# Depthwise convolution by stacks in both layers, a second tile for the sums made on GpSimd, and a third bank of exponentials ahead of a long activation

## The chip, the cores and the metric

The kernel runs on one core of a Trainium2 chip. All eight images of the batch are worked on by this one core, one after the other. The metric is device time in microseconds; the runs shown are three, and their median is what the change is measured against. One further execution was profiled, and everything said below of single instructions is from that one.

The engines are named as in the profile: PE is the matrix engine (TensorE), PEld its weight loads, DVE is VectorE, ACT is ScalarE, POOL is GpSimd, SP is the engine that issues the DMAs.

## The reference, cut to what matters

The input is eight images of 56 x 56 points with 192 channels, in float32. Each layer adds its result to its input, and each is applied to a group norm of its input (32 groups of 6 channels).

```python
# layer 0: attention on separable convolutions
x = x + L0(gn(x))
#   q  = pointwise(batchnorm(depthwise3x3(xn, dw_q,  stride 1)))      3136 queries
#   kv = pointwise(batchnorm(depthwise3x3(xn, dw_kv, stride 2)))       784 keys
#   o  = softmax(q k^T / 8) v     (3 heads of 64), then out_w, out_b

# layer 1: a selective scan in four directions
x = x + L1(gn(x))
#   xa, z = split(xn @ in_proj)                 384 channels each
#   xc = silu(depthwise3x3(xa) + conv_b)
#   for four directions k (rows, columns, and both reversed):
#     dt, B, C = split(xs @ x_proj[k]);  delta = softplus(dt @ dt_proj[k] + bias[k])
#     h = exp(delta * A) * h + delta * B * u     # 384 channels x 16 states, 3136 points
#     y = sum over the 16 states of h * C
#   out = (layernorm(sum of the four y, plus the skip) * silu(z)) @ out_proj
```

## The kernel before, in words

The points of an image are cut into seven chunks of 448 (`T`), that is eight rows of 56. The 384 channels of the scan are three blocks of 128 partitions (`NJ`).

**The scan** is the main loop. A step is one image, one direction and one chunk; there are 8 x 4 x 7 = 224 steps of 16 states each. For each state of a step:

- `inputs_made` (L1165, POOL): h = du x B for 128 x 1344 elements, into one of seven tiles h (`HBUFS`).
- `decays` (L1179, ACT): three exponentials da, each into a PSUM bank.
- `scans` (L1196, DVE): three scans of 448 elements, h = da x h + input; `carries` (L1218) keeps the last column.
- For most states PE turns h round (`turned`, L1242, 12 transposes), ACT scales the result by C (`scaled`, L1258), and PE turns it back into the sum y (`back`, L1276).
- For four states of a step (three in the last image) POOL multiplies by C instead (`by_pool`, L1294) and adds up in a tile `yp` (L1298): two groups of states to a step. PE adds each finished group to y (`summed`, L1313). The tile `yp` exists once; the first product of a group can be written only when PE has read the group before.
- DVE adds y to the image's sum `yacc` (L1330 and L1328).

**What goes before and after an image's scan.** `front(b)` is layer 0 and the beginning of layer 1 for image b. It turns the input round and takes the statistics (L519 to L534), then loads normalised bands of ten rows (L576) and convolves them: `dgkv` and `dgq` are diagonal 96 x 96 matrices, one for each of nine taps and two channel blocks, and each tap is a matmul on the shifted band (L634 for keys and values with 112 columns, L471 for queries with up to 448). The pointwise products follow (L651 to L665), then the attention (`attend`, L775 and L784, with the exponentials at L725), the product with out_w (L756), a second group norm, and the in-projection of layer 1 (L890). Layer 1's depthwise convolution goes by *stacks* (L908): a stack holds the same rows three times, shifted by one image row, on 3 x 32 partitions, so that one matmul with 32 output channels does three taps; four such matmuls, for four groups of 32 channels, write four quarters of the PSUM partitions. A silu over 3136 elements ends it (`stored`, L870). `x_proj(b)` makes delta, B and C (L982 to L999) with one Softplus for every two directions of a chunk (L958). `finish(b)` is the layer norm, the gate with a silu of its own (L1063) and the output product.

**The order of the work.** Each of these is a Python generator that asks for an engine with an estimated cost, what it reads and what it writes. A planner (`Sched.run`) keeps an estimated time for each engine and always takes the request that could start first; what comes out is one fixed order of instructions on each engine, the DMAs on SP's queue among them. All engines take their queues in order. While image b is scanned, `front(b+1)` and `x_proj(b+1)` are woven in; `pace` holds the estimated PE time that they have used to a share that grows with the scans done, within 12 us. When PE has nothing to do by the planner's estimate, it is given filler matmuls (L1408). The front of image 0 stands ahead of the first scan and overlaps with nothing.

**PSUM.** During the scan y takes three banks. Five banks are shared by name: at most two for the exponentials (`rda`), two for turned states (`rht`) and one for everything in `front`, `x_proj` and `finish` (`bank1`).

**Weights** of the pointwise products, of out_w, of x_proj and of dt_proj (`pwq`, `pwkv`, `outw0`, `outw1`, `xpw`, `dtw`) stay in SBUF for the whole run.

Of the kernel before, what the change touches and what calls it, by code (L numbers as in the profile page):

```python
# [18 lines left out]
L = HW * HW  # L19
# [26 lines left out]
LEAD = 3  # L46

# [226 lines left out]
def kernel(  # L274
# [54 lines left out]
    pwq = fill("pwq", [CP, NB, 256], 0.0)  # L329
    nc.sync.dma_start(pwq[:, :, 0:C], pw_q.rearrange("(b p) d -> p b d", p=CP))  # L330
    pwkv = load("pwkv", [CP, NB, 2 * C], pw_kv.rearrange("(b p) d -> p b d", p=CP))
    outw0 = load("outw0", [128, C], out_w[0:128, :])
    outw1 = fill("outw1", [128, C], 0.0)
    nc.sync.dma_start(outw1[0:64, :], out_w[128:192, :])
# [3 lines left out]
    xpw = fill("xpw", [128, 2, NJ, 2, 64], 0.0)  # L338
    for k in range(NDIR):
        nc.sync.dma_start(xpw[:, k % 2, :, k // 2, :NR], xp_wT[k].rearrange("(j p) r -> p j r", p=128))  # L340

    dtw = fill("dtw", [128, NDIR, DIN], 0.0)
    for k in range(NDIR):
        nc.sync.dma_start(dtw[k // 2 * 64:k // 2 * 64 + R, k], dt_wT[:, k, :])
# [37 lines left out]
    dgq_d = dconst.tile([CP, NB, 9, CP], F32, name="dgq_d")  # L382
    dgkv_d = dconst.tile([CP, NB, 9, CP], F32, name="dgkv_d")
    dgx_d = dconst.tile([96, NJ, 4, 3, 32], F32, name="dgx_d")
    xpd = [dconst.tile([128, NJ, HW + 2, HW + 2], F32, name=f"xpd{i}") for i in range(2)]
    for t in xpd:
        for row in (0, HW + 1):
            nc.sync.dma_start(t[:, :, row], zeros[:, :HW + 2].unsqueeze(1).to_broadcast([128, NJ, HW + 2]))
    with tc.tile_pool(name="taps", bufs=2) as taps:
        for dst, src, p, nb in ((dgq_d, dw_q, CP, NB), (dgkv_d, dw_kv, CP, NB)):  # L390
            w = taps.tile([p, nb, 9], F32, name="w")
            nc.sync.dma_start(w, src.rearrange("(b p) t -> p b t", p=p))
            for bl in range(nb):
                d = taps.tile([p, 9, p], F32, name="d")
                for t in range(9):
                    nc.vector.tensor_scalar(d[:, t], ident[:p, :p], w[:, bl, t:t + 1], None, ALU.mult)
                nc.sync.dma_start(dst[:, bl], d)


        id3 = taps.tile([96, 32], F32, name="id3")  # L400
        w3 = taps.tile([96, NJ, 4, 3], F32, name="w3")
        for dy in range(3):
            rows = slice(32 * dy, 32 * dy + 32)
            nc.vector.tensor_copy(id3[rows], ident[rows, rows])
            nc.sync.dma_start(w3[rows].rearrange("c j g x -> c (j g) x"),
                              conv_w[:, 3 * dy:3 * dy + 3].rearrange("(q c) x -> c q x", c=32))
        for j in range(NJ):
            d = taps.tile([96, 4, 3, 32], F32, name="d3")
            for g in range(4):
                for dx in range(3):  # L410
                    nc.vector.tensor_scalar(d[:, g, dx], id3, w3[:, j, g, dx:dx + 1], None, ALU.mult)
            nc.sync.dma_start(dgx_d[:, j], d)
# [4 lines left out]
    s1 = Rings(ctx.enter_context(tc.tile_pool(name="s1", bufs=1)), 1)  # L417
# [44 lines left out]
    TAPS = (4, 0, 1, 2, 3, 5, 6, 7, 8)  # L462

    def conv_rows(out, lhs, img, row0, rows, t):


        dy, dx = divmod(t, 3)
        lo, hi = max(row0 + dy - 1, 0), min(row0 + dy - 1 + rows, HW)
        o0, o1 = lo - (row0 + dy - 1), hi - (row0 + dy - 1)
        a, b = max(0, 1 - dx), min(HW, HW + 1 - dx)  # L470
        nc.tensor.matmul(out[:, o0:o1, a:b], lhs, img(lo, hi)[:, :, a + dx - 1:b + dx - 1],  # L471
                         start=(t == TAPS[0]), stop=(t == TAPS[-1]))

# [18 lines left out]
    def front(b):  # L492
# [13 lines left out]
        with tc.tile_pool(name=f"fx_{b}", bufs=2) as pool:  # L506
            fx = Rings(pool, 2)
            k_st = [Cell() for _ in range(NCH)]

            def part(c):  # L510
# [3 lines left out]
                xt = yield fx("xt", [CP, NB, T], parts=NB)  # L514
# [13 lines left out]
                yield from dma(xt.c, [k_xr[c]], 3.8, xr[:, :, cols], xt.ap, [xt])  # L528
# [5 lines left out]
            nc.vector.scalar_tensor_tensor(off, mean, -1.0, rstd, ALU.mult, ALU.mult)  # L534

        with tc.tile_pool(name=f"kv_{b}", bufs=1) as kvp:
# [18 lines left out]
            with tc.tile_pool(name=f"fd_{b}", bufs=1) as fd:  # L555
                fe = Rings(fd, 1)
                dgq = fd.tile([CP, NB, 9, CP], F32, name="dgq")
                dgkv = fd.tile([CP, NB, 9, CP], F32, name="dgkv")
                k_dq, k_dk = Cell(), Cell()
                yield from dma([], [k_dk], 7.4, dgkv, dgkv_d)  # L560
                yield from dma([], [k_dq], 5.7, dgq, dgq_d)
                s_q, t_q = bns["q"]
                s_kv, t_kv = bns["kv"]
                bands, ends = {}, []

                def load_bands():
                    for c in range(NCH):
                        base = c * RPC - 1
                        r0, r1 = max(base, 0), min(base + BR, HW)
                        band = yield fe("band", [CP, NB, BR, HW], parts=3)  # L570
                        bv = band.ap[:, :, r0 - base:r1 - base]
                        yield from dma(k_xr[max(c - 1, 0):c + 2], [band.c[2]], 4.5, bv,
                                       xr.rearrange("p b (h w) -> p b h w", w=HW)[:, :, r0:r1])
                        for bl in range(NB):
                            yield ACT, t_act(BR * HW), [band.c[2], k_gn], [band.c[bl]]
                            nc.scalar.activation(bv[:, bl], bv[:, bl], AF.Identity, bias=off[:, bl:bl + 1],  # L576
                                                 scale=rstd[:, bl:bl + 1])
                        bands[c] = band
# [37 lines left out]
                def convs():  # L616
                    for c in range(NCH):
                        base = c * RPC - 1
                        yield lambda: c in bands
                        band = bands[c]  # L620


                        hkv = yield fe("hkv", [CP, NB, TP], parts=NB)
                        hq = yield fe("hq", [CP, NB, T], parts=NB)
                        for bl in range(NB):
                            pk = yield bank()
                            pkv = pk.ap[:CP, :TP].rearrange("p (h w) -> p h w", w=KW)
                            for t in range(9):
                                dy, dx = divmod(t, 3)
                                nr = 4 if c * RPC + 6 + dy < HW else 3  # L630
                                ncol = KW if dx < 2 else KW - 1
                                if t % 3 == 0:
                                    yield PE, 3 * t_mm(TP), [band.c[bl], k_dk], pk.c if t == 6 else []
                                nc.tensor.matmul(pkv[:, :nr, :ncol], dgkv[:, bl, t],  # L634
                                                 band.ap[:, bl, 1 + dy:1 + dy + 2 * nr - 1:2, dx:dx + 2 * ncol - 1:2],
                                                 start=(t == 0), stop=(t == 8))
                            sc.spawn(kv_out(pk, hkv, bl))
# [533 lines left out]
    def decays():  # L1171
        for i, n in todo:
# [8 lines left out]
            if n == NST - 1:  # L1181
                dl.free()
# [297 lines left out]
```

## Time and profile before

| | |
|---|---|
| three runs, us | 17917.75, 17898.47, 17909.62; median 17909.62 |
| the profiled execution's own time, us | 17887.45 |
| its span on the core, us | 17885.7 |
| granted PE clock | 0.974 |
| busy, us: PE, DVE, ACT, POOL | 16160.6, 14114.4, 14223.1, 15550.4 |
| PE filler matmuls (L1408), us | 1423.6 |
| first POOL input of the scan, us from the start | 742.2 |
| DMA traffic | 2306.95 MB, 129 GB/s on average |

Three stretches follow one another. Up to about 740 us stands the front of image 0. Then come seven periods, each with the scan of one image and the front of the next; bands are loaded at 11866.5 and again at 14043.5 us, so that a period is some 2170 us long. From about 16,150 us on the last image is scanned with no front beside it. A row of a table of stretches gives the stretch and its length, then the busy time and the number of instructions of PE, PEld, DVE, ACT and POOL, the granted PE clock, the DMA engines' share and the GB/s. A row of waits gives the waiting line, what it waited for, the sum in us, how often, and the longest.

### The profile page before, as it was taken

Reading aid. Unit: us, or ns where it says so; the run is one execution under the profiler, and the core shown is the slowest. Engines: PE = TensorE matmul, PEld = TensorE weight load, DVE = VectorE, ACT = ScalarE, POOL = GpSimd, SP = SyncE. Lnnn points to the kernel's source line nnn. Section 1 sums busy time; section 2 is a strip of 40 time slices with the busy share of each in tenths; the row PEclk is TensorE's granted clock in tenths of the full one; section 3 lists DMA queues with packets and bytes.
Section 4 is the critical chain, followed back from the end, with each engine's and each line's share of the span. In section 5 each row is a group of like instructions: output and inputs, shape, how many; then the busy total and the mean of one; then the engine's idle time right before and its main releaser. Section 6 shows DMA issues by size and latency. Waiting matters only on the chain. (4 is left out here: it accounts for less than half of the span.)

```text
span 17885.7 us, 277600 instructions
## 1 busy us (share of the span) xinstructions
PE 16160.6 (90%) x99800; PEld 11302.8 (63%) x99800; DVE 14114.4 (79%) x17839; ACT 14223.1 (80%) x25030; POOL 15550.4 (87%) x5200
## 2 busy tenths in 40 slices
PE   8699989998899989999899998999989999899998
PEld 4366656666666666666566665666656666667776
DVE  2378878888778887788787887878878788788898
ACT  2478878787877878788787887878878788888888
POOL 0388889898898989899898998989979899899998
PEclk9799999999999999999999999999999999999999
DMA  1643365334553355533554336543364433643332
GB/s 51 183 151 93 101 182 168 108 99 123 173 165 97 95 140 166 158 99 98 155 156 152 100 97 168 155 139 102 95 179 155 129 100 98 190 151 115 95 100 79
DMA packets 1461825, 2306.95 MB, mean 129 GB/s; under 512 B 189264, under 2 KB 1447776, under 8 KB 1457376
## 3 DMA queue, kind: packets, MB, share of 16 engines
q1 hardware_dynamic: 1460448, 2289.19, 43.6%
q8 instruction: 791, 12.96, 0.3%
q14 instruction: 586, 4.80, 0.1%
HBM read 1758.53 MB, written 530.15 MB: 128 GB/s over the span
## 5 line engine op out<-in xcount | busy, mean ns | idle before, releaser
L1196 DVE TENSOR_TENSOR_SCAN h<-da,newc,h 128x448 f32<-128x448 f32 x9216 | 10077.2, 1136 | 1781.7 <-ACT da L1179 1184.3
L1165 POOL TENSOR_TENSOR h<-du_s,bb 128x1344 f32<-128x1344 f32 x3584 | 10818.6, 3052 | 613.8 <-PE ht L1242 502.2
L1258 ACT ACTIVATE g<-ht,ct_s 112x384 f32<-112x384 f32 x10864 | 5928.9, 577 | 1596.5 <-PE ht L1242 1386.1
L1179 ACT ACTIVATE da<-dl_s,acoef 128x448 f32<-128x448 f32 x10752 | 6582.2, 636 | 741.1 <-DVE h L1196 391.6
L1276 PE MATMUL y<-ident,g 112*128 112x112 f32 x32592 | 4865.3, 268 | 649.4 <-ACT g L1258 458.7
L1242 PE MATMUL ht<-ident,h 128*112 128x128 f32 x32592 | 5181.5, 277 | 221.5 <-DVE h L1196 136.2
L1276 PEld LDWEIGHTS y<-ident,g 112*128 112x128 f32 x32592 | 3556.7, 142 | 2648.2 <-ACT g L1258 1569.1
L1242 PEld LDWEIGHTS ht<-ident,h 128*112 128x112 f32 x32592 | 3679.2, 135 | 847.1 <-DVE h L1196 392.8
L1196 DVE TENSOR_TENSOR_SCAN h<-da,h 128x448 f32<-128x448 f32 x1536 | 1590.9, 1076 | 394.7 <-ACT da L1179 258.6
L1294 POOL TENSOR_TENSOR yp<-h,cb 128x1344 f32<-128x1344 f32 x448 | 1366.4, 3050 | 452.2 <-PE y L1313 262.0
L1294 POOL TENSOR_TENSOR h<-h,cb 128x1344 f32<-128x1344 f32 x420 | 1281.0, 3050 | 311.2 <-DVE newc L1218 166.9
L1408 PE MATMUL y<-zeros 128*128 128x64 f32 x10568 | 1423.6, 274 | 0.0
L1408 PEld LDWEIGHTS y<-zeros 128*128 128x128 f32 x10568 | 1377.1, 198 | 49.0 <-issue 49.0
L966 POOL TENSOR_TENSOR v<-v,xs 128x1344 f32<-128x1344 f32 x224 | 677.1, 3044 | 761.4 <-DMA dl<-v 696.0
L1298 POOL TENSOR_TENSOR yp<-yp,h 128x1344 f32<-128x1344 f32 x420 | 1279.4, 3046 | 32.7
L1313 PE MATMUL y<-yp,ident 128*128 128x448 f32 x2688 | 1208.5, 546 | 3.1 <-POOL yp L1294 1.8
L775 PE MATMUL bank<-qT,kT 128*112 128x448 f32 x2352 | 1057.3, 570 | 130.5 <-DVE oT L738 78.3
L784 PE MATMUL bank<-pT,vt 112*128 112x448 f32 x2352 | 1006.2, 546 | 16.6 <-ACT pT L725 8.1
L725 ACT ACTIVATE pT<-bank,nsh 112x448 f32<-112x448 f32 x1176 | 742.0, 633 | 156.6 <-PE bank L775 117.8
L471 PE MATMUL bank<-band,dgq 96*96 96x440 f32 (+3 forms) x2016 | 823.6, 532 | 21.7 <-ACT hq L601 7.0
L775 PEld LDWEIGHTS bank<-qT,kT 128*112 128x112 f32 x2352 | 365.3, 178 | 537.0 <-issue 142.3
L999 PE MATMUL bank<-xd,dtw 128*128 128x448 f32 x1344 | 626.5, 572 | 33.3 <-DVE sz L1060 8.8
(149 smaller groups left out, 10790.4 us busy)
## 6 DMA issues: line engine op xcount, KB each, us to landing
bb<-rows SPq DMA_DIRECT2D x3584, 224.0 KB, 3.3
cb<-rows SPq DMA_DIRECT2D x868, 224.0 KB, 3.6
dl<-v SPq DMA_DIRECT2D x224, 672.0 KB, 4.9
du<-v SPq DMA_DIRECT2D x224, 672.0 KB, 5.5
du_s<-du SPq DMA_DIRECT2D x224, 672.0 KB, 4.6
dl_s<-dl SPq DMA_DIRECT2D x224, 672.0 KB, 4.9
stack<-xpd SPq DMA_DIRECT2D x504, 232.0 KB, 4.7
xt<-x1d SPq DMA_DIRECT2D x224, 336.0 KB, 5.2
```

Of the source, the lines that this page charges most:

```text
L775: nc.tensor.matmul(ps.ap[:TP, :T], kts[h][:, kb * TP:(kb + 1) * TP], qh.ap, start=True, stop=True)
L784: nc.tensor.matmul(po.ap[:, :T], vt[:, kb, g:g + 2, :].rearrange("p g d -> p (g d)"), pts[kb].ap, start=(kb == 0), stop=(kb == NKB - 1))
L1165: nc.gpsimd.tensor_tensor(h.ap, du.ap, bb.ap.unsqueeze(1).to_broadcast([128, NJ, T]), ALU.mult)
L1179: nc.scalar.activation(da.ap[:, :T], dl.ap[:, j], AF.Exp, scale=acoef[:, k * NJ + j, n:n + 1])
L1196: nc.vector.tensor_tensor_scan(h.ap[:, j, rev], da.ap[:, 0:T][:, rev], h.ap[:, j, rev], news[i - 1].ap[:, j, n:n + 1] if ci else 0.0, ALU. ...
L1242: nc.tensor.transpose(ht.ap[:TP, j * 128:(j + 1) * 128], h.ap[:, j, s * TP:(s + 1) * TP], ident)
L1258: nc.scalar.activation(g.ap, ht.ap[:TP, :DIN], AF.Copy, scale=ct.ap[:, s, n:n + 1])
L1276: nc.tensor.matmul(y["t"].ap[:, j, s * TP:(s + 1) * TP], g.ap[:, j * 128:(j + 1) * 128], ident[:TP, :TP], is_transpose=True, start=(n == 0 ...
L1294: nc.gpsimd.tensor_tensor(to.ap, h.ap, cbr.ap.unsqueeze(1).to_broadcast([128, NJ, T]), ALU.mult)
L1298: nc.gpsimd.tensor_tensor(yp.ap, yp.ap, h.ap, ALU.add)
L1313: nc.tensor.matmul(y["t"].ap[:, j, :T], ident, yp.ap[:, j], start=False, stop=(y["left"][j] == 0))
L1408: nc.tensor.matmul(ybanks[:, 0, T:T + FILL], zeros, zeros[:, :FILL], start=False, stop=False)
```

## The change

- **Layer 0's convolution** also goes by stacks. After the group norm's statistics the image is normalised chunk by chunk (`normal`, ACT) into a tile with a zero column on each side, and stored to a padded image in DRAM (`xnd`, its first and last row zeroed once). `load_stacks` reads a stack for each chunk and channel block with three DMAs; three stacks are kept (`STACKS`). Keys and values take nine matmuls for a block, queries nine; the weights are 96 x 32 blocks. The bands, their normalisation and the 96 x 96 diagonals are gone.
- **Two tiles `yp`** in place of one.
- **`long_act`** stands around the two silus and the Softplus. It raises the limit of `rda` to three banks and lets the planner place the long activation only when three exponentials for coming scans have been placed (`stocked`); afterwards the limit is two again.
- **Weights** for layer 0, out_w, x_proj and dt_proj are no longer kept: they are laid out once, written to DRAM, and loaded into a pool of each phase of each image.

```diff
+STOCK = 3
+STACKS = 3
...
-    s1 = Rings(ctx.enter_context(tc.tile_pool(name="s1", bufs=1)), 1)
...
             def part(c):
...
-                xt = yield fx("xt", [CP, NB, T], parts=NB)
+                xt = yield fx("xt", [CP, NB, T], NCH, parts=NB)
+                xts[c] = xt
...
+            def normal(c):
+                pad = yield rpad
+                for bl in range(NB):
+                    yield ACT, t_act(T), [xts[c].c[bl], k_gn], [pad.c[bl]]
+                    nc.scalar.activation(pad.ap[:, bl, :, 1:HW + 1], xts[c].ap[:, bl].rearrange("p (h w) -> p h w", w=HW),
+                                         AF.Identity, bias=off[:, bl:bl + 1], scale=rstd[:, bl:bl + 1])
+                xts[c].free()
+                yield from dma(pad.c, [k_xn[c]], 3.8, xn.rearrange("(b p) h w -> p b h w", p=CP)[:, :, 1 + c * RPC:1 + (c + 1) * RPC],
+                               pad.ap, [pad])
...
+            yield from sc.join([sc.spawn(normal(c)) for c in range(NCH)])
...
-                def load_bands():
+                def load_stacks():
                     for c in range(NCH):
...
                         for bl in range(NB):
-                            yield ACT, t_act(BR * HW), [band.c[2], k_gn], [band.c[bl]]
...
+                            st = yield fe("stack", [96, 3, RPC * (HW + 2)], STACKS, parts=3)
+                            for dy in range(3):
+                                src = xn[bl * CP:(bl + 1) * CP, c * RPC + dy:(c + 1) * RPC + dy].rearrange("(g q) h w -> q g (h w)", q=32)
+                                yield from dma(k_xn[max(c - 1, 0):c + 2], [st.c[dy]], 3.5, st.ap[32 * dy:32 * dy + 32], src)
+                            stacks[c, bl] = st
...
                             pk = yield bank()
-                            for t in range(9):
...
+                            yield PE, 3 * t_mm(TP) + 0.1, st.c + [k_w], pk.c
+                            for dx in range(3):
+                                for g in range(3):
+                                    nc.tensor.matmul(pk.ap[32 * g:32 * g + 32, :TP].rearrange("p (h w) -> p h w", w=KW),
+                                                     dgkv[:, bl * 3 + g, dx], sv[:, g, 1:RPC:2, dx + 1:dx + HW:2],
+                                                     start=(dx == 0), stop=(dx == 2))
...
                             pq = yield bank()
-                            for t in TAPS:
-                                yield PE, t_mm(T), [band.c[bl], k_dq], pq.c if t == 8 else []
...
+                            for dx in range(3):
+                                yield PE, t_mm(T), st.c + [k_w], pq.c if dx == 2 else []
+                                for g in range(3):
+                                    nc.tensor.matmul(pq.ap[32 * g:32 * g + 32, :T].rearrange("p (h w) -> p h w", w=HW),
+                                                     dgq[:, bl * 3 + g, dx], sv[:, g, :, dx:dx + HW],
+                                                     start=(dx == 0), stop=(dx == 2))
+                            st.free()
...
+    def stocked():
+        if not rdas or at["decay"] not in chunks:
+            return True
+        made = sum(t.busy and t.by is rdas[0] and t.c[0].w is not None for t in rdas[0].tiles)
+        return made >= STOCK
+
+    def long_act(cost, reads, writes):
+
+        at["long"] += 1
+        if rdas:
+            rdas[0].most = STOCK
+        yield stocked
+        yield ACT, cost, reads, writes
+        at["long"] -= 1
+        if rdas and not at["long"]:
+            rdas[0].most = 2
...
-                yield ACT, t_act(L) + 2.6, xv.c, [k1]
+                yield from long_act(t_act(L) + 2.6, xv.c, [k1])
                 nc.scalar.activation(xv.ap, xv.ap, AF.Silu)
...
-                yield ACT, 2 * t_act(NJ * T) + 2.6, v.c, [k_sp]
+                yield from long_act(2 * t_act(NJ * T) + 2.6, v.c, [k_sp])
                 nc.scalar.activation(v.ap, v.ap, AF.Softplus)
...
-            yield ACT, t_act(NJ * T) + 2.6, sz.c[1:1 + NJ], [sz.c[1 + NJ]]
+            yield from long_act(t_act(NJ * T) + 2.6, sz.c[1:1 + NJ], [sz.c[1 + NJ]])
             nc.scalar.activation(sz.ap, sz.ap, AF.Silu)
...
-                yp = yield s1("yp", [128, NJ, T])
+                yp = yield s2("yp", [128, NJ, T])
...
+                outw, k_ow = pool.tile([128, 2, C], F32, name="outw", bufs=1), Cell()
+                yield from dma([], [k_ow], 3.0, outw, outw_d)
...
+            xpw, dtw, k_w = pool.tile([128, 2, NJ, 2, 64], F32, name="xpw", bufs=1), pool.tile([128, NDIR, DIN], F32, name="dtw", bufs=1), Cell()
+            yield from dma([], [k_w], 4.0, xpw, xpw_d)
+            yield from dma([], [k_w], 5.0, dtw, dtw_d)
```

## Prediction, on record before the change was run

> **What bounds the kernel now.** I read first the busy table of the whole run, then a table of stretches over one image's period (8640 to 10800 us), then POOL's waits in that period.
>
> ```profile
> PE 16160.6 (90%) x99800; PEld 11302.8 (63%) x99800; DVE 14114.4 (79%) x17839; ACT 14223.1 (80%) x25030; POOL 15550.4 (87%) x5200
> ```
>
> ```profile
> 8640.00:8800.00 160.00, 137.53 (x773) 96.70 (x774) 138.92 (x171) 105.24 (x194) 128.19 (x43) 0.89 0.62 169
> 8800.00:9040.00 240.00, 212.96 (x1613) 142.91 (x1601) 155.17 (x194) 194.44 (x312) 188.15 (x63) 0.96 0.70 200
> 9040.00:9600.00 560.00, 517.45 (x3118) 365.77 (x3117) 466.39 (x592) 475.32 (x780) 540.89 (x180) 0.99 0.49 153
> 9600.00:9760.00 160.00, 140.46 (x879) 111.84 (x877) 113.30 (x159) 95.39 (x167) 111.65 (x42) 0.89 0.50 157
> 9760.00:10080.00 320.00, 298.94 (x1937) 216.10 (x1935) 269.36 (x349) 262.35 (x484) 312.11 (x104) 1.00 0.35 103
> 10080.00:10160.00 80.00, 64.36 (x366) 43.86 (x365) 73.32 (x86) 54.70 (x102) 66.05 (x23) 0.89 0.31 92
> 10160.00:10800.00 640.00, 601.33 (x3455) 401.07 (x3455) 535.17 (x659) 570.79 (x1058) 606.84 (x202) 1.00 0.35 97
> ```
>
> The rows are: in-projection; layer 1's convolution with its silus; x_proj with the finish of the image before; input and first norm; layer 0's convolution; norms of keys; attention. POOL's busy time is the fifth pair. It is 97% busy in x_proj, 98% in the convolution, 95% in attention, and 70 to 83% in the others. In the last image, where there is no front, POOL is 100% busy. So POOL is the floor: 22 operations of 3.01 us per step, 66.3 us, 28 times, with 28 products in x_proj and 7 in finish, make 1962 us of a period of 2160. The change takes nothing from POOL. It can win only from POOL's 206 idle us per period: 84 in the first two rows, 19 in x_proj, 48 at the first norm, 8 in the convolution, 14 at the keys' norms, 33 in attention. Who caused them:
>
> ```profile
> POOL h L1165 <- PE ht L1242: 61.2, 17, 12.3
> POOL yp L1294 <- PE y L1313: 22.3, 12, 5.0
> POOL yp L1294 <- DVE h L1196: 20.1, 3, 16.3
> POOL h L1294 <- DVE newc L1218: 19.9, 6, 8.1
> POOL h L1294 <- issue: 16.1, 8, 4.8
> POOL h L1165 <- DVE qe L610: 10.6, 1, 10.6
> POOL yp L1294 <- DMA stack<-xpd: 10.0, 1, 10.0
> ```
>
> The first row is POOL waiting for a free tile h. The second is the one tile yp; so is the last, where PE's reading of yp stood in its queue behind a convolution whose stack had not landed.
>
> The exposed front of image 0 is different: there PE is the bound, and these rows price the two kinds of convolution.
>
> ```profile
> 86.28 3.86 PE L634 MATMUL bank<-band,dgkv 96*96 96x112 f32 x36 [0.56 <-ACT band L576]
> 89.98 13.53 PE L471 MATMUL bank<-band,dgq 96*96 96x448 f32 x36
> ...
> 522.05 4.72 PE L908 MATMUL bank<-stack,dg 96*32 96x448 f32 x48
> ```
>
> ```profile
> 13159.66 6.97 PE L908 MATMUL bank<-stack,dg 96*32 96x448 f32 x48 [4.31 <-DMA stack<-xpd]
> ```
>
> By bands two query blocks take 13.4 us. By stacks two blocks of four groups take 4.65 us (to the next start at 526.70).
>
> **What the Trainium skill says.** "TensorEngine Tiling (Array Packing)", Key Properties: different tiles load weights and multiply in parallel. The trace agrees: 24 instructions of 448 columns go in 2.33 us, about six times the 0.37 us that one took in the band convolution (13.4 / 36). "TensorE: Matmul & The Clock Gate", Part 1: after an idle window of about 3.4 us PE runs at half rate. The trace agrees: after 4.31 us of idling the same 48 instructions took 6.97 us in place of 4.72. "ScalarE: Activation LUTs", What ACT_TABLE_LOAD costs: some 1.28 us each; the trace has 1283 ns, twice for each long activation. "DMA: Bandwidth & Descriptors", Anatomy of one DMA: a DMA's semaphore wait is held by the issuing sequencer. So a stack load that waits for a free stack holds what SP has queued behind it.
>
> **The change, part by part.**
>
> 1. *The convolution on PE.* Queries keep six groups of passes (three dx, two passes): 2.3 us for a block in place of 6.7, 8.8 us less per chunk. Keys and values have 112 columns: between 0.64 us (six groups at 0.107, the old time of one instruction) and 1.93 us (no overlap, no saving) for a block; I take 0.9, 2.1 us less per chunk. Together 10.9 us per chunk, 76 per image, 610 in all. Only the exposed image has it on its path.
>
> 2. *Image 0, exposed.* Seven chunks fall from 22.3 us (86.28 to 108.53) to 11.4: -76. Against this stands the longer way from the norm to the first convolution, 7.5 us before (54.64 to 62.17). Now seven chunks are normalised into two pads: 14 activations at 0.72 us (L601's time for the same 96 x 448), and each pad is free again after 1.4 + 0.6 + 4.7 us (the landing of xr<-xt, the same size), so seven take 7 x 6.7 / 2 = 23.5. Then four weight loads are issued (2.2) and a stack lands (4.7): 31 us, +24. Writing the padded weights at the start puts some 20 DMAs between the input loads on SP, at 0.45 us and a few landings: 0 to 20, I take 10. Sum -42.
>
> 3. *The overlapped convolutions.* They lie under POOL's 98%, so 76 us less PE work there win nothing directly. But the pace is counted in PE time. The built program's order shows what becomes of it, counted in scans (48 to a step) on DVE for a middle image: layer 0's convolution shrinks from 268 to 106, attention goes from 455 to 525, x_proj from 359 to 398. In attention the step is now 640 / 441 x 48 = 69.7 us against POOL's 66.3, with PE at 94%; spread over 70 scans more it has some 3 us less PE work per step. Of the 33 us of idling there, the 8 that wait for ht, and part of the "issue", go: I take 12 us per image, bounds 0 to 22.
>
> 4. *Two tiles yp.* The waits for L1313 are 262.0 us in the run, those by way of a late stack 41.0: 303, or 43 per image; 32 in this period. POOL's order confirms the effect: before, a group's first product often stands directly ahead of the second; after, four or five inputs lie between them. POOL then runs ahead and meets the next limit, the seven tiles h, which already cost 61 us here. I keep half to two thirds: 25, bounds 5 to 43.
>
> 5. *The third bank.* A silu holds ACT for 2.82 + 2 x 1.28 = 5.4 us, a Softplus 5.0. DVE waits 52.8 us for exponentials between 8720 and 9040. Two exponentials cover 2.3 us of scans, three 3.4; and often not even two were ready. So 1.1 to 3.4 us per long activation. For the 14 Softplus this is hidden: POOL is at 97% there. For three silus and some of the seven gates it shows: 12 us per image. The price is that a long activation waits for its stock and what needs it (DMAs of xcs, products of POOL) comes later, and that five banks are asked for six times: -2 to +20 in all. I take 10.
>
> 6. *What the change adds to a period.* After the norm, the front has the longer way of part 2, and falls behind its pace. The order on PE shows what follows: eight convolution blocks and the pointwise products of three chunks almost in one piece, 8 x 3.2 + 3 x 5.0 = 40 us, with only some eight turns of states between; before, the piece was one chunk, 22 us. POOL can run ahead of PE by seven tiles, 21 us, so it stands for up to 19 us where it stood for about 1. DVE has the same 26 us of small work for layer 0 (hkv, vt, qe, qm by their rows) in 2 steps in place of 5, some 72 us per step there. I take 10 us for both, bounds 0 to 30. Stack loads are 42 more DMAs per image; SP issues one in about 0.55 us, 23 us beside 150: nothing, unless they wait for a free stack.
>
> Per period: 12 + 25 + 10 - 10 = 37, and 5 of the 53 us of waits for ht outside attention, where PE has less queued: 42. Seven periods: -294. The last image: 0, POOL is already full. With image 0: -336. The profiled execution took 17887.45 us, so 17551; the median of the runs is 22 above it: 17573, say 17570.
>
> **Rivals.**
>
> *All of it counts.* yp keeps its 43, PE relief 20, silus 20, and the block after the norm costs 5: 78 per period, 546, and 60 from image 0: 17909 - 606, about 17300. For it: no other engine is above 85% without fillers. Against: POOL's waits for ht.
>
> *The waits only move.* POOL runs ahead and waits for h instead; the period wins 5 us and image 0 its 42: 17909 - 77, about 17830. For it: the largest row of waits is that for h. Against: attention and x_proj hardly wait for it.
>
> *Slower, by the block of convolutions.* After each first norm PE works 40 us for the front alone, first at half clock if it idled; the stacks, three deep, have to be loaded within it, and SP holds the bb rows behind them. If this costs POOL more than the 42 us won, the whole is slower; at 72 us per period it is +30 x 7 - 42, about 18080. For it: before, the stretch around this norm already was the slowest (160 us for 78 scans). Against: 21 us of states lie ready, and bb has three tiles.
>
> **The numbers.** Forecast 0.47; all of it 0.20; only moved 0.18; slower 0.15. The range 17230 to 17890 takes in the first three cases (0.85) but for some 5 in 100 beyond its ends: 0.8. This kernel's measurement can tell 0.2% (36 us) from no change. Faster by more: 0.47 + 0.20 + 0.13 of the third = 0.80; within: 0.06; slower: 0.14.
>
> **What would show it.** POOL's waits at yp for L1313 near zero; a stack block of queries at about 2.3 us, of keys at 0.7 to 1.2; POOL's first input of the scan near 700 us in place of 742; attention's step at 67 to 68 us; POOL's wait for ht just after each first norm. A key block at 1.9 us, a period above 2160, or a start of the scan after 742 would prove me wrong.

## The result, and the profile after

The changed kernel takes 17707.39 us (median; 17692.75 to 17731.28) beside 17906.77 us (17898.47 to 17917.75) for the kernel before: ratio 0.989, 95% interval 0.9872 to 0.9907. It is 199 us faster; 336 had been forecast. The profiled execution has a span of 17729.6 us, 156 less than before, and is itself the longest of the runs shown. So of the 199 us the two traces can show only about 156.

The busy table of the changed kernel:

```profile
PE 15852.5 (89%) x101500; PEld 11102.4 (63%) x101500; DVE 14151.2 (80%) x17871; ACT 14191.9 (80%) x25030; POOL 15551.3 (88%) x5200
```

PE has lost only 308 us, though by its chunk time (below) some 650 of the convolutions are gone: 214.6 came back as fillers (L1441: 1638.2 in place of 1423.6); the rest I did not trace. POOL's work is the same, as it must be; its idle time is what counts.

Image 0 first. PE and then POOL at its front (time, duration, instruction, number; in brackets the idle time before it and what ended it):

```profile
54.63 0.45 PE L460 MATMUL bank<-dm,group 96*96 96x2 f32 x2 [0.92 <-DVE dm L457]
82.12 1.34 PE L640 MATMUL bank<-stack,dgkv 96*32 96x112 f32 x18 [27.03 <-DMA stack<-xnd]
83.21 4.72 PE L648 MATMUL bank<-stack,dgq 96*32 96x448 f32 x18
...
95.96 0.83 PE L640 MATMUL bank<-stack,dgkv 96*32 96x112 f32 x18
96.60 2.44 PE L648 MATMUL bank<-stack,dgq 96*32 96x448 f32 x18
98.86 0.81 PE L640 MATMUL bank<-stack,dgkv 96*32 96x112 f32 x18
99.48 2.44 PE L648 MATMUL bank<-stack,dgq 96*32 96x448 f32 x18
106.58 0.83 PE L640 MATMUL bank<-stack,dgkv 96*32 96x112 f32 x18
```

```profile
69.20 1.41 ACT L539 ACTIVATE pad<-xt,off,rstd 96x448 f32<-96x448 f32 x2 [1.37 <-DMA xnd<-pad]
```

```profile
685.54 14.90 POOL L1195 TENSOR_TENSOR h<-du_s,bb 128x1344 f32<-128x1344 f32 x5 [12.38 <-DMA bb<-rows]
```

The last matmul of the statistics starts at 54.63 in place of 53.40, so the 20 DMAs at the start cost at most 1.2 us. The first convolution starts at 82.12 in place of 62.17. The first query block after 27.03 us of idling takes 4.72 us; from the second chunk on, a query block takes 2.25 us (96.60 to 98.86, block start to block start), a key block 0.64, and a chunk 10.6 us (95.96 to 106.58) where it took 22.3. POOL's first input comes at 685.5 in place of 742.2.

Then the seven periods. These are stretches over the scan of one middle image, cut by scans on DVE (48 scans are a step): steps 0 to 3, 4 to 7, 8 to 15, 16 to 21, 22 to 27; each cut lies 4 to 13 us ahead of its step's first scan. The columns are those of the prediction's table.

```profile
7249.00:7607.00 358.00, 323.17 (x2278) 228.13 (x2277) 279.37 (x385) 256.83 (x450) 293.25 (x102) 0.96 0.56 163
7607.00:7898.00 291.00, 268.20 (x1631) 183.66 (x1630) 250.97 (x307) 246.93 (x459) 270.19 (x91) 0.98 0.35 100
7898.00:8435.00 537.00, 497.12 (x2949) 338.84 (x2948) 461.50 (x568) 480.47 (x894) 524.62 (x175) 1.00 0.34 96
8435.00:8946.00 511.00, 437.17 (x2967) 302.10 (x2965) 389.27 (x477) 390.52 (x653) 425.15 (x142) 0.94 0.64 184
8946.00:9398.00 452.00, 417.33 (x2623) 302.95 (x2623) 385.69 (x483) 387.39 (x657) 448.00 (x150) 0.99 0.46 140
```

Steps 8 to 15 and 16 to 21 of the same image in the kernel before:

```profile
8015.00:8574.00 559.00, 526.13 (x3032) 351.98 (x3030) 470.37 (x579) 497.64 (x922) 526.29 (x176) 1.00 0.35 98
8574.00:9073.00 499.00, 442.87 (x2936) 303.75 (x2937) 380.24 (x467) 388.50 (x664) 413.03 (x138) 0.95 0.61 173
```

The attention (third row) has POOL at 98% in place of 94% in the same steps before, x_proj (last row) at 99% in place of 98%. The fourth row, where the second norm, the in-projection, layer 1's convolution and the first part of x_proj lie, is the slow one: POOL 83% busy and 86 us idle, the same as before. The next table gives the mean over images 1 to 5, in us, from the start of a step's first scan to the start of the next group's first scan in each trace:

| kernel | steps 0-3 | 4-7 | 8-15 | 16-21 | 22-27 | sum |
|---|---|---|---|---|---|---|
| before | 351.5 | 287.8 | 560.1 | 504.9 | 470.7 | 2175.0 |
| changed | 358.4 | 289.4 | 541.7 | 519.4 | 457.7 | 2166.6 |

These images gained some 8.5 us each. Over all seven periods the gain is 15.4 on average, since image 0's is 46 us shorter and image 6's 20; 42 had been forecast. POOL's waits over the whole run say where the promise of the second tile went. First come groups of the kernel before (busy time, mean ns of one, then the idle time before them), then the waits of the changed kernel:

```profile
L1294 POOL TENSOR_TENSOR yp<-h,cb 128x1344 f32<-128x1344 f32 x448 | 1366.4, 3050 | 452.2 <-PE y L1313 262.0
L1294 POOL TENSOR_TENSOR h<-h,cb 128x1344 f32<-128x1344 f32 x420 | 1281.0, 3050 | 311.2 <-DVE newc L1218 166.9
```

```profile
POOL h L1195 <- PE ht L1274: 436.8, 173, 15.3
POOL h L1326 <- issue: 410.1, 79, 23.2
POOL yp L1326 <- issue: 153.1, 36, 21.7
POOL h L1326 <- DVE newc L1250: 118.7, 32, 13.7
POOL yp L1326 <- DVE h L1228: 108.1, 51, 11.9
```

The waits of yp for PE's sum (262.0 us before) are gone. But the products (L1326), which multiply a state that DVE must have scanned, now wait 790 us in the four rows of L1326, where before the rows of the same kinds (L1294) held 390. With all rows the products wait 868 us in place of 763. The row "h <- issue" stands for DVE too: in each of its waits the semaphore that came last is that of the column which DVE carries on (L1250). Of the row "yp <- issue" most is DMAs.

### The profile page after: what moved, and what is told of

It reads as the page before. It is cut to its first block, busy times and chain, and to the rows that moved or that the text cites. A ratio compares the mean times of both kernels' runs of the same rounds, so it can differ in the third digit from the quotient of the medians.

```text
span 17729.6 us, 282518 instructions
## 1 busy us (share of the span) xinstructions
PE 15852.5 (89%) x101500; PEld 11102.4 (63%) x101500; DVE 14151.2 (80%) x17871; ACT 14191.9 (80%) x25030; POOL 15551.3 (88%) x5200
## 5 line engine op out<-in xcount | busy, mean ns | idle before, releaser
L1195 POOL TENSOR_TENSOR h<-du_s,bb 128x1344 f32<-128x1344 f32 x3584 | 10823.5, 3054 | 527.5 <-PE ht L1274 436.8
L1308 PE MATMUL y<-ident,g 112*128 112x112 f32 x32592 | 4920.5, 270 | 626.4 <-ACT g L1290 450.7
L1326 POOL TENSOR_TENSOR h<-h,cb 128x1344 f32<-128x1344 f32 x420 | 1282.0, 3052 | 583.4 <-issue 410.1
L1441 PE MATMUL y<-zeros 128*128 128x64 f32 x12268 | 1638.2, 270 | 0.0
L1441 PEld LDWEIGHTS y<-zeros 128*128 128x128 f32 x12268 | 1581.0, 196 | 60.5 <-issue 60.5
L1326 POOL TENSOR_TENSOR yp<-h,cb 128x1344 f32<-128x1344 f32 x448 | 1367.2, 3052 | 284.8 <-issue 153.1
L792 PE MATMUL bank<-pT,vt 112*128 112x448 f32 x2352 | 1018.8, 544 | 26.0 <-ACT pT L733 21.8
L1013 DVE TENSOR_SCALAR v<-bank,dtb 128x448 f32<-128x448 f32 x672 | 456.2, 679 | 264.1 <-PE bank L1010 249.7
```

The costliest lines, as they stand in the source:

```text
L792: nc.tensor.matmul(po.ap[:, :T], vt[:, kb, g:g + 2, :].rearrange("p g d -> p (g d)"), pts[kb].ap, start=(kb == 0), stop=(kb == NKB - 1))
L1195: nc.gpsimd.tensor_tensor(h.ap, du.ap, bb.ap.unsqueeze(1).to_broadcast([128, NJ, T]), ALU.mult)
L1308: nc.tensor.matmul(y["t"].ap[:, j, s * TP:(s + 1) * TP], g.ap[:, j * 128:(j + 1) * 128], ident[:TP, :TP], is_transpose=True, start=(n == 0 ...
L1326: nc.gpsimd.tensor_tensor(to.ap, h.ap, cbr.ap.unsqueeze(1).to_broadcast([128, NJ, T]), ALU.mult)
L1441: nc.tensor.matmul(ybanks[:, 0, T:T + FILL], zeros, zeros[:, :FILL], start=False, stop=False)
```

## The experiments

**Which part is worth what.** Four kernels: the change with one yp; without the stock of exponentials; with only the convolutions (both undone); and the kernel before with nothing but the stock.

```diff
-                yp = yield s2("yp", [128, NJ, T])
+                yp = yield s2("yp", [128, NJ, T], 1)
```

```diff
     def long_act(cost, reads, writes):
-        at["long"] += 1
-        if rdas:
-            rdas[0].most = STOCK
-        yield stocked
         yield ACT, cost, reads, writes
-        at["long"] -= 1
-        if rdas and not at["long"]:
-            rdas[0].most = 2
```

> The changed kernel with one tile yp again; all else as changed. Theory 1, the sum on record: the second tile is worth 25 us per period, so this is 175 us slower than the changed kernel, about 17880. Theory 2, the waits only moved (after the change POOL waits 868 us ahead of all products in place of 763, though hardly any for PE's reading of yp): it is within 40 us of the changed kernel, 17670 to 17750, and POOL's waits for PE at yp come back while those at the second product shrink.

> The changed kernel with the long activations placed as before the change: at most two banks of exponentials, no waiting for a stock. Theory 1, the sum on record: 10 us per period are lost, 70 us slower than the changed kernel, about 17780. Theory 2: the stock wins in the steps with Softplus and gates (steps 22 to 27 of a period became 14 us shorter) and loses about as much where the silus stand (steps 16 to 21 became 15 us longer, as five banks are asked for six times), so it is within 40 us. If the stock only costs, this is some 100 us faster, about 17600.

> Only the convolutions by stacks (with the weights reloaded): one yp and no stock. Theory 1: the start 42 to 57 us earlier, 12 us per period from a lighter PE, 10 lost to the block of convolutions after the norm: some 70 us faster than before, 17840. Theory 2, the stacks alone carry the gain: start 57 us earlier, attention 18 us per period shorter, norm and convolution 9 longer: 57 + 9 x 7 = 120 us faster, 17790; what is then left of the 200 is of the two other parts together.

> The kernel before with the third bank and the stock ahead of each long activation alone. Theory 1: 10 us per period, 17840. Theory 2: within 40 us of the kernel before, 17870 to 17950; the silus' steps longer, the Softplus' and gates' steps shorter.

| kernel | us | ratio to before (95%) |
|---|---|---|
| convolutions alone | 17732.28 | 0.9897 (0.9883 to 0.9912) |
| and two yp, no stock | 17659.60 | 0.9859 (0.9844 to 0.9874) |
| and stock, one yp | 17751.84 | 0.9908 (0.9892 to 0.9924) |
| changed kernel (all three) | 17707.39 | 0.9890 (0.9872 to 0.9907) |
| before and stock | 17928.94 | 1.0007 (0.9998 to 1.0015) |

The convolutions alone are worth 182 us, more than either expectation. The second yp adds 73 without the stock and 44 with it, though there the intervals overlap. The stock takes 48 back (the two intervals overlap slightly; the stages below speak for it too), 20 with one yp, where the intervals overlap widely, and is worth nothing in the kernel before. Without it the changed kernel would be better than it is.

POOL's waits account for the 73 us. First with the convolutions alone, then with two yp as well (there the products are L1319, the sum of yp on PE L1338):

```profile
POOL h L1188 <- PE ht L1267: 527.7, 161, 18.7
POOL yp L1319 <- PE y L1338: 235.1, 90, 32.2
POOL h L1319 <- DVE newc L1243: 225.0, 80, 12.7
POOL h L1319 <- issue: 146.7, 38, 18.6
POOL yp L1319 <- DVE h L1221: 95.2, 28, 11.9
```

```profile
POOL h L1188 <- PE ht L1267: 507.8, 159, 18.3
POOL h L1319 <- DVE newc L1243: 248.2, 60, 13.7
POOL h L1319 <- issue: 194.2, 50, 21.2
POOL yp L1319 <- DVE h L1221: 157.7, 75, 9.1
```

All the idle time before the products is in their groups, again first with one yp:

```profile
L1319 POOL TENSOR_TENSOR yp<-h,cb 128x1344 f32<-128x1344 f32 x448 | 1367.2, 3052 | 426.4 <-PE y L1338 235.1
L1319 POOL TENSOR_TENSOR h<-h,cb 128x1344 f32<-128x1344 f32 x420 | 1281.5, 3051 | 395.6 <-DVE newc L1243 225.0
```

```profile
L1319 POOL TENSOR_TENSOR h<-h,cb 128x1344 f32<-128x1344 f32 x420 | 1282.6, 3054 | 477.4 <-DVE newc L1243 248.2
L1319 POOL TENSOR_TENSOR yp<-h,cb 128x1344 f32<-128x1344 f32 x448 | 1366.6, 3050 | 264.8 <-DVE h L1221 157.7
```

235.1 us of waits for PE vanish, but the sum falls only from 822 to 742, by 80 us, beside 73 measured. The other 155 us came back as other waits of the same products. Sorted by the semaphore that came last, some 90 of them are waits for DVE's scans and carried columns, some 60 for DMAs. All waits of L1188 together stay the same (601.0 and 602.3), though those for PE's turns fall by 19.9.

**What the stock costs, and where.** By stages (images 1 to 5), without and with the stock: steps 22 to 27 are 12.3 us shorter with it (470.0 to 457.7), as it was meant, but steps 16 to 21 are 21.8 longer (497.6 to 519.4), 13.6 of them in step 21 alone. There DVE stands at the scaling of the gate's weights (L476). DVE, then POOL, in the changed kernel:

```profile
8883.77 0.14 DVE L1250 TENSOR_REDUCE newc<-h 128x3 f32<-128x3 f32 x1
8883.83 11.70 DVE L476 TENSOR_SCALAR wz<-wz,rstd 96x384 f32<-96x384 f32 x2
8895.45 0.67 DVE L1013 TENSOR_SCALAR v<-bank,dtb 128x448 f32<-128x448 f32 x1
8896.05 2.05 DVE L1228 TENSOR_TENSOR_SCAN h<-da,h 128x448 f32<-128x448 f32 x2
```

```profile
8883.01 11.98 POOL L1195 TENSOR_TENSOR h<-du_s,bb 128x1344 f32<-128x1344 f32 x4
8905.41 3.05 POOL L1326 TENSOR_TENSOR h<-h,cb 128x1344 f32<-128x1344 f32 x1 [10.42 <-issue]
```

Two instructions that take 0.4 us each when POOL is idle (404 ns is the shortest in this trace) take 11.70 us together and end 0.5 us after POOL's four inputs; nearly all of it is one instruction, since the longest takes 11412 ns. The scans stand behind them, POOL's product needs one of these scans, and so POOL then idles for 10.42 us. So it is once in each of images 1 to 6. Without the stock POOL's work at the same place is no less dense, but each of the pair stands for one operation of POOL only, 6.2 us together:

```profile
8872.23 6.23 DVE L476 TENSOR_SCALAR wz<-wz,rstd 96x384 f32<-96x384 f32 x2
```

```profile
8866.02 6.10 POOL L1188 TENSOR_TENSOR h<-du_s,bb 128x1344 f32<-128x1344 f32 x2
8872.02 3.10 POOL L1319 TENSOR_TENSOR h<-h,cb 128x1344 f32<-128x1344 f32 x1
8875.21 3.04 POOL L1323 TENSOR_TENSOR yp<-yp,h 128x1344 f32<-128x1344 f32 x1
```

That POOL is what holds them shows in the ends: of the 48 scalings of wx and wz in the changed kernel 22 took over 1 us, and all 22 end 0.21 to 0.22 us after the end of an operation of POOL. Six of them stood through four operations, the other 16 to the end of one, at times with POOL's next operation following at once. What decides between one and four isn't shown. Other small DVE instructions on SBUF stand likewise in the changed kernel: the centring of kT (L697, up to 10.7), the copy of the mean (L455, up to 12.3), km (L701, up to 1.9). The Trainium skill ("SBUF — State Buffer", Who interferes with whom) says that tensor_scalar in its two-port mode, and tensor_tensor with both inputs in SBUF, contend for a pair of ports that GpSimd also uses, and that the second to start is blocked until the first ends; tensor_reduce does not contend. The trace agrees with the list: L1250 took 0.14 us beside POOL, and L1013, which reads PSUM, 0.65. In the length it agrees for the 16 that stood to the end of one POOL operation of 3.0 us, and differs for the six that stood through four.

The first test keeps the order and makes these instructions tensor_tensor with a broadcast operand; the mean is read from PSUM.

```diff
-        nc.vector.tensor_copy(mean, gm[:, :, 0])
+        nc.vector.tensor_copy(mean, pg.ap[:CP, 0:2 * NB].rearrange("p (b s) -> p b s", s=2)[:, :, 0])
...
-            nc.vector.tensor_scalar(w[:, bl], w[:, bl], rstd[:, bl:bl + 1], None, ALU.mult)
+            nc.vector.tensor_tensor(w[:, bl], w[:, bl], rstd[:, bl:bl + 1].to_broadcast([CP, DIN]), ALU.mult)
```

> The changed kernel, the order of every engine kept, with four small DVE operations in another form: the scaling of wx and wz, the centring of the keys and their products with the maxima as tensor_tensor on a broadcast operand in place of tensor_scalar, and the copy of the mean from PSUM in place of SBUF. In the trace these last up to 11.7 us beside POOL (wz 3.55 us on average, mean 2.62, keys 2.19) and 0.4, 0.17 and 0.63 at the front of image 0 where POOL is idle. Theory 1 (DVE stands until POOL's run of operations ends, and all scans with it): each takes its short time, some 190 us of DVE time come free, 27 per period, and the kernel is 60 to 190 us faster, about 17590. Rival (it is only DVE time beside a POOL that is busy anyway): within 40 us.

> The same four operations in the other form, in the changed kernel without the stock. Theory 1 (the stock's 48 us are mostly the scaling of wz, which its order of work puts ahead of four operations of POOL, 11.7 us, and without it ahead of two, 6.2): the difference between stock and no stock shrinks from 48 to under 20 us, and this is about 17580. Rival (the third bank itself takes room from the convolution and x_proj): the difference stays, this is about 50 us under the run with the stock and the same form.

17697.32 us (0.9884, 0.9869 to 0.9899) and 17679.77 us (0.9874, 0.9861 to 0.9888): neither differs from the kernel that it came from by more than the intervals. The stock's difference shrank to 18 us as theory 1 had it, but not by its mechanism, since the two kernels stand at 17697 and 17680, not at the 17590 and 17580 expected. The groups of DVE show why, first of the changed kernel, then of this one (sum and mean ns of one):

```profile
L476 DVE TENSOR_SCALAR wz<-wz,rstd 96x384 f32<-96x384 f32 x32 | 112.4, 3552 | 0.2 <-DMA wz<-in_in_wT_dram 0.2
```

```profile
L476 DVE TENSOR_TENSOR wz<-wz,rstd 96x384 f32<-96x384 f32 x32 | 119.2, 3763 | 0.0
```

The other form stands just as long. Only the mean was freed. So this test did not test the theory. The second puts the same work on ScalarE, at the same places in the order:

```diff
-            nc.vector.tensor_scalar(w[:, bl], w[:, bl], rstd[:, bl:bl + 1], None, ALU.mult)
+            nc.scalar.activation(w[:, bl], w[:, bl], AF.Copy, scale=rstd[:, bl:bl + 1])
...
-                nc.vector.tensor_scalar(ks, ks, 1.0 / KEYS, None, ALU.mult)
+                nc.vector.tensor_scalar(ks, ks, -1.0 / KEYS, None, ALU.mult)
...
-                nc.vector.tensor_scalar(kt, kt, ks, None, ALU.subtract)
+                nc.scalar.activation(kt, kt, AF.Identity, bias=ks)
...
-                nc.vector.tensor_scalar(km, qms[h // 2], kx, None, ALU.mult)
+                nc.scalar.activation(km, qms[h // 2], AF.Copy, scale=kx)
```

> The changed kernel with the order of all work kept, but VectorE's small scalings issued on ScalarE at the same places: wz and wx (L476), the centring of kT (L697) and km (L701); the mean is copied from PSUM. In the trace of the changed kernel these instructions stand on VectorE until POOL's run of operations ends (wz 11.7 us each, kT up to 10.7, km up to 1.9), some 35 us in each of seven periods. Theory (this standing is what the stock costs and more): 60 to 190 us faster than the changed kernel, about 17590 us. Rival (VectorE's standing is hidden behind waits for POOL anyway, or returns as waits on ScalarE): within 40 us of it, 17670 to 17750 us.

> The same edit in the changed kernel without the third bank made ahead. There wz stands 6.2 us instead of 11.7. If wz's standing is what the stock costs, the difference of 48 us between stock and no stock shrinks to under 20 us between after_act and this one, and this one is about 17580 us. Rival (the stock costs by its work or by its place on ScalarE): the difference stays 35 to 60 us.

17519.23 us (0.9783, 0.9770 to 0.9797) and, without the stock, 17587.47 us (0.9816, 0.9802 to 0.9829). The changed kernel gains 188 us; the one without the stock 72. The stock, which cost 48 us, now gains 68, and these two intervals do not touch. By stages: with the scalings on ScalarE, steps 16 to 21 take 494.5 us with the stock and 497.3 without it (with them on DVE the stock's were 21.8 longer), while the gain in steps 22 to 27 stays (457.4 and 469.1). The same stretch of POOL in the changed kernel with the scalings on ScalarE:

```profile
8781.10 12.07 POOL L1195 TENSOR_TENSOR h<-du_s,bb 128x1344 f32<-128x1344 f32 x4
8793.13 3.04 POOL L1326 TENSOR_TENSOR h<-h,cb 128x1344 f32<-128x1344 f32 x1
```

After the same four inputs the product follows without a gap. The expectation for the second kernel (the difference shrinks to under 20) was still too cautious: it turned round. Its mechanism is shown for the group of moved instructions: the stock's cost was DVE's standing, not its work on ScalarE. That wz alone is the cause isn't shown, since the keys' scalings and the mean moved with it. The kernel with one yp fits: no wz there stood longer than 3.2 us, and the stock's 20 us are not clear of the noise.

**The block of convolutions.** In the changed kernel PE works at the front's convolutions in nearly one piece from 7462.29 to 7513.4 in a middle image (four of the seven chunks), with single turns of states in between. Two kernels were to break it up: one that lets the front fall further behind its pace, and one that lowers the head start (`URGENT`) by which a late front is placed ahead of the scan's work.

```diff
-                return want + 12.0, want - 12.0
+                return want + 12.0, want - 60.0
```

```diff
-URGENT = 0.9
+URGENT = 0.4
```

> The changed kernel with one number of the pace changed: the front may lag by 60 us of PE time, in place of 12, before it is put ahead of the scan. So the convolutions after the first norm needn't come in one piece. Theory 1 (the block of part 6 costs 16 to 20 us per period, step 2 of a period being 94 us in place of 74): about 120 us faster than the changed kernel, 17590. Rival (the block's cost is the longer way from the norm to the first convolution, or what is put off comes back elsewhere in the period): within 40 us, 17670 to 17750.

> The changed kernel with the planner's URGENT at 0.4 in place of 0.9, which breaks the block of convolutions after each norm up: the y products and h/t sums of the scan come in between the key and query blocks. Theory (the block of about 50 us on TensorE starves POOL and eats the gain of the convolutions, step 2 of a period 74 to 94 us): step 2 back to about 75, 15 to 20 us in each of seven periods, 100 to 140 us faster than the changed kernel, about 17600 us. Rival (only the place of the work within the period moved, what step 2 loses other steps had lost before): within 40 us of the changed kernel or slower.

The first took 17794.64 us (0.9940, 0.9927 to 0.9952). The convolutions moved some two steps later, the block stayed a block; it says nothing on the block, only that a later front costs 87 us. The second took 17384.85 us (0.9704, 0.9691 to 0.9718), 322 us faster than the changed kernel and three times what I had expected. The block is loosened: the image's first eight key blocks take 76 us (from 7341.0) in place of 49 (from 7462.3). All fourteen take 135 in place of 151, so the convolution as a whole isn't spread out further. But the gain is not there. By stages:

| kernel | steps 0-3 | 4-7 | 8-15 | 16-21 | 22-27 | sum |
|---|---|---|---|---|---|---|
| changed | 358.4 | 289.4 | 541.7 | 519.4 | 457.7 | 2166.6 |
| changed, URGENT 0.4 | 345.5 | 307.0 | 537.3 | 479.4 | 449.8 | 2119.0 |
| before, URGENT 0.4 | 392.7 | 294.5 | 561.7 | 497.0 | 442.8 | 2188.8 |

Around the block (steps 0 to 7) nothing was won: 647.7 and 652.5 us. What steps 0 to 3 win, steps 4 to 7 lose. Most of the gain lies in steps 16 to 21, whose convolution and in-projection are the same before and after. I took that for an advantage that the kernel before must have too, and tried it:

> The kernel before the change with URGENT at 0.4 in place of 0.9. In the changed kernel this gave 322 us, but by steps only step 2 of the block of convolutions got better (94.0 to 78.7), steps 3 to 7 lost it again (sum of steps 0 to 7: 651 and 655 us), and the gain lay in steps 16 to 21 (519 to 475), where the second norm, the in-projection and layer 1's convolution are the same before and after. If so, the kernel before gains 200 to 350 us, about 17630 us. Rival (the changed kernel's convolutions in one piece are what URGENT mends): less than 80 us, above 17830.

17928.15 us, ratio 1.0003 (0.9995 to 1.0011). It has none, and that conclusion from the stages fell: in images 1 to 5 it wins 36 us in steps 16 to 27 and loses 48 in steps 0 to 7. POOL's waits of the kernel before with URGENT at 0.4, over the whole run:

```profile
POOL yp L1294 <- PE y L1313: 589.8, 100, 53.6
POOL h L1165 <- PE ht L1242: 412.4, 96, 19.9
```

And of the changed kernel with URGENT at 0.4:

```profile
POOL h L1326 <- issue: 340.6, 60, 15.0
POOL h L1195 <- PE ht L1274: 224.3, 95, 7.3
```

In the kernel before, the waits for a free h fall by 90 us (from 502.2), and those of the one yp for PE's sum rise by 328 (from 262.0). In the changed kernel with URGENT at 0.4 the second kind is nearly gone (7 us in images 1 to 5), and the first falls from 436.8 to 224.3. This suggests that the two tiles are at least part of what the lower head start needs; the changed kernel with one yp and URGENT at 0.4, which would show it, was not run. Whether two tiles are enough, or the short convolutions are needed too, these runs do not tell apart: the kernel before lacks both.

**Both together.** The scalings on ScalarE and URGENT at 0.4:

> The changed kernel with both: VectorE's small scalings on ScalarE (188 us by itself) and URGENT at 0.4 (322 by itself). If both take different waits they add up, about 17200 us. If both take the same idle time of POOL in steps 16 to 21 (after_act took some 33 us there, URGENT 44), it ends near 17350, within 50 of URGENT alone. I take about 17270.

17284.61 us, ratio 0.9643 (0.9630 to 0.9656): 423 us faster than the changed kernel, of 510 if the two simply added up, and close to the 17270 expected. It is the fastest version here.

## Why the prediction came out as it did

The sign, the bound (POOL) and the range held. The size did not: 199 us in place of 336, because two terms of the period's sum were wrong. The steps in turn:

1. **Convolution on PE: held.** A query block 2.25 us (2.3 forecast), a key block 0.64 (0.9; it is the lower bound of the range given, just under the 0.7 named as a sign), a chunk 10.6 (11.4).
2. **Image 0: held, somewhat too small.** The scan starts 57 us earlier (745.2 to 688.6 for DVE's first scan), 42 forecast. The seven chunks gave 7 x (22.3 - 10.6) = 82, the longer way from the norm and the DMAs at the start cost 20 together (82.12 - 62.17), not 24 + 10; the 5 us between 82 - 20 and 57 I did not trace. Normalising ended at 70.6, some 15 us after the norm, not 23.5, and the DMAs at the start cost at most 1.2.
3. **PE relief in attention: held, somewhat too small.** Steps 8 to 15 won 18.0 us with the convolutions alone and 18.4 with the whole change; 12 forecast, up to 22. The step is 67.7 us (67 to 68).
4. **Two tiles yp: the term that was mis-sized.** I kept 25 of 43 us per period. Images 1 to 5 won 8.5 (2162.2 with the convolutions alone, 2153.7 with two yp), all seven periods 11.4 on average, the whole run 73. The waits at L1313 vanished as forecast; what stood behind them was named wrongly. I expected the seven tiles h to be next. Their wait for PE fell. Next was the product itself: 155 of the 235.1 us came back as its other waits, most of them for DVE's scans, the rest mainly for DMAs. My "POOL then runs ahead" was the error: an earlier product is one that has to wait for its scan.
5. **The third bank: wrong sign.** Forecast +10 us per period, measured -13 in images 1 to 5 (2153.7 to 2166.6) and -8.5 over all seven periods. The medians, 48 us apart, say -7; the profiled execution is the longest of its runs with the stock and the shortest without. A gain exists, 12 us, but in steps 22 to 27, where the Softplus lie, which I had called hidden. The cost was outside my bounds (-2 at worst), since I priced only the stock's own waiting. In the moved order DVE's scaling of wz stood through four operations of POOL in place of one. Nothing in the change names this instruction; but its group in the trace of before (L481 there, 405 to 3199 ns for one instruction) showed that it is held up by something, as did the copy of the mean (L448 there, up to 9458 ns), and I did not look at them.
6. **The block after the norm: inside its bounds, cause not settled.** With the convolutions alone steps 0 to 3 lost 4.9 us (10 forecast for the block, bounds 0 to 30). Loosening the block did not make steps 0 to 7 shorter, so it isn't shown that the block as such costs it.

The terms in the order of the runs, mean of the seven periods in the traces: convolutions 12.5 (12 - 10 + 5 = 7 forecast), second yp 11.4 (25), stock -8.5 (10): 15.4 in place of 42. Part of the error was made good by terms that were forecast too small: image 0's start by 15 us and the convolutions by 5 a period. Of the rivals, "the waits only move" was half right: it names the wrong place (h), but two thirds of the yp's waits did move. "Slower, by the block" did not happen; image 0's period, with the front of image 1 in it, became 46 us shorter (2278 to 2233).

## What to carry to other kernels

Before a wait is counted as won, ask what the freed instruction needs next: here POOL's earlier product mostly met the scan that it multiplies. After a change of order, look at the small instructions that the busiest engine holds up on another; a pair worth 0.8 us stood for 11.7 and turned the sign of one part of the change, and moving it and its like elsewhere (188 us) was worth nearly as much as the whole change (199). And a knob of the planner (`URGENT`) is to be tried again after a change: a lower value was worth nothing before the change and 322 us after it.

## What was not expected of the hardware

DVE instructions with all operands in SBUF stood beside POOL until an operation of POOL ended: mostly one of 3.0 us, but six of 48 scalings through a run of four back to back (11.70 us beside 11.98 for the pair). Tensor_scalar and tensor_tensor stood alike (means of 3552 and 3763 ns over 32; 404 is the shortest). Whether one operation or the run ends the wait, these traces don't settle. The same scaling on ScalarE takes 599 to 616 ns beside the same POOL. A copy of 96 x 2 elements took up to 12.3 us when read from SBUF and 146 ns when read from PSUM.
